# A new gate for the work that is threaded between state-space scans: own ScalarE time, due time of the next decay, and new TensorE figures in the planner

## Chip, core and metric

The kernel runs on one core of a Trainium2 chip. The metric is device time in microseconds (us) of one execution; the median of three runs is used, and 0.3% is about the least difference that they can tell. A core has TensorE (matrix products into PSUM), VectorE, ScalarE (functions by table) and GpSimd; SyncE issues the DMAs. Each engine takes its instructions in the order in which the program gives them and waits at each for what it needs, so an instruction that waits also holds up all those behind it.

## The reference

Four layers act on four images of 96 channels and 64 x 64 pixels (4096 positions).

- Layer 0: layer norm, projection to 2 x 192 channels, a 3 x 3 depthwise convolution with silu, then a selective scan of 192 channels x 16 states in 4 directions (by rows, by columns, and both backwards), the sum of the four, a layer norm, a gate, a projection, and an MLP with gelu.
- Layer 1: group norm, a smaller convolution and scan in two directions with one state a channel, gate, projection.
- Layer 2: a Fourier transform along the positions with a pointwise complex layer, and an MLP with its values rounded to FP8.
- Layer 3: linear attention (no softmax) and the same MLP.

The scan of layer 0 is where most of the time goes. Cut to what matters:

```python
dt = softplus(x_dbl[dt rows] @ dt_projs_w + bias);  A = -exp(A_logs)
def step(hst, inp):                          # for every position, in order
    dA = exp(dt_t[..., None] * A)            # the decay
    hst = hst * dA + dt_t[..., None] * B_t * x_t[..., None]
    y_t = sum over the 16 states of hst * C_t
```

## The kernel before

**Tiles of the scan.** A tile holds 32 channels x 4 states on 128 partitions and 1024 positions. For 4 images, 4 directions (in the order 0, 1, 3, 2), 4 chunks of 1024 positions and 24 tiles a chunk there are 1536 tiles. In `scan` (from line 655) the work on tile i is spread over the engines:

- GpSimd multiplies u by B into `w` (`input_of`, L745), three tiles ahead; there are nine `w` buffers.
- ScalarE makes the decay exp(dt A) into `h` (`decay`, an activation whose trace line is L144), two tiles ahead; there are two `h` buffers.
- VectorE runs the scan (L821), with `h` and `w` as inputs.
- The product with C is done on VectorE (L829) for most tiles and on GpSimd (L841) for 5 of 24 tiles of image 0 and 8 of 24 of the others (`POOL_OUT`, `pool_out`). The last state is copied by ScalarE (L837) or GpSimd (L834).
- TensorE sums over the states, for two tiles at once (`sums`, L767, into `py`), and VectorE adds `py` to `y` once in eight tiles (`add_sums`, L779 and L782).

**The stream.** All the other layers are written as generators, which end each of their steps with `yield`: `front(b)` (layer norm, convolution, step sizes of layer 0, stored in DRAM for the scan), `weights`, and `rest(b)`, which is `tail` (end of layer 0), `l1`, `transform`, `middle` and `back`. They stand in one queue, `stream`, and `step()` runs the front one to its next `yield`. `run` takes tasks in groups of w; beside the scan w is 1, so one task is in flight. It waits until 8 us (`LANDED`) of planned time have passed since the loads of a group were issued. `rest(b)` is queued when the last direction of image b begins, and its tail can take a part of the image only when that direction's scan has passed it. `need` runs steps without a gate when the scan needs a front that isn't there.

**The planner.** The order of instructions is fixed while the program is built. `now` holds the planned time of each engine and `chain` the planned end of the stream's last work on it. `spend` charges a stream operation to an engine behind what it needs, and `tick` charges the scan's work: 2.35 us for a scan, 1.23 for a product on VectorE, 1.12 for a decay, 2.36 for GpSimd's products. An activation costs 0.25 us plus 0.86 ns for each element of a partition, and 2.6 us more where the function table changes. A matmul costs what `mm` (L97) says, divided by `side` where it fills only part of the array. `later` puts a VectorE operation of the stream off, and `flush` issues it when the planned time of VectorE has reached that of its inputs; as long as one is put off no further step is taken.

**The gate.** After the scan of a tile, and again at the end of the tile, `advance` (from line 1543) decides whether one step of the stream is run there. It compares how far TensorE's chain, ScalarE, GpSimd and TensorE are ahead of the time `free`, and takes one step if the latest is at most 2 us (first place, `FIRST`) or 1 us (second, `SECOND`) beyond it:

```python
late = max(chain["pe"] - 0.5, now["act"], now["pool"] - 6.0, now["pe"] - 2.0) - free
if not put_off and late <= slack:
    step()
```

The scan starts when the first chunk's inputs are there. When it has ended, what is left of `rest(3)` runs with eight PSUM banks and up to four tasks at once, without the gate.

Of the kernel before, what the change touches and what calls it, by code (L numbers as in the profile page):

```python
# [11 lines left out]
F32 = mybir.dt.float32  # L12
# [17 lines left out]
POOL_OUT = (5, 8, 8, 8)  # L30
# [2 lines left out]

LANDED = 8.0

FIRST, SECOND = 2, 1
ENGINES = ("pe", "act", "dve", "pool")


# [17 lines left out]
def tile_hybrid(ctx: ExitStack, tc: tile.TileContext, I: dict, out: bass.AP):  # L57
# [5 lines left out]
    now, chain = (dict.fromkeys(ENGINES, 0.0) for _ in range(2))  # L63
    done_at, used, slot_of = {}, {}, {}

    def tick(e, us, *behind):
        now[e] = max(now[e], 0.0, *behind) + us
        return now[e]

    def blocks(ap):  # L70
        t = ap.tensor
        if ap.space == DRAM:
            return []
        span = sum(abs(st) * (n - 1) for st, n in list(ap.ap)[1:])
        lo = ap.offset % int(np.prod(t.shape[1:]))
        return [(t.name, q) for q in range(lo // 512, (lo + span) // 512 + 1)]

    def spend(e, us, reads=(), writes=()):
        behind = [chain["dve"]]
        for ap in reads:  # L80
            behind += [done_at.get(q, 0.0) for q in blocks(ap)]
        for ap in writes:
            behind.append(used.get(slot_of.get(ap.tensor.name), 0.0))
        chain[e] = end = tick(e, us, *behind)
        for ap in writes:
            for q in blocks(ap):
                done_at[q] = end
        for ap in (*reads, *writes):
            if ap.tensor.name in slot_of:
                used[slot_of[ap.tensor.name]] = end  # L90

    def size(ap):
        return int(np.prod(ap.shape[1:]))

    def mm(o, lhsT, rhs, side=1, **kw):

        spend("pe", size(rhs) / side * (2.4e-3 if rhs.dtype == F32 else 1.2e-3), (lhsT, rhs), (o,))  # L97
        nc.tensor.matmul(o, lhsT=lhsT, rhs=rhs, **kw)  # L98

    dve = nc.vector  # L100
    pool = nc.gpsimd
# [30 lines left out]
    def act(o, i, func, own=False, **kw):  # L132

        if func in (AF.Exp, AF.Ln):
            if table[0] != "ln exp":
                nc.scalar.preload_act_table_set("natural_log_exp_and_others")  # L136
            table[0] = "ln exp"
        elif func in (AF.Silu, AF.Gelu, AF.Softplus):
            if table[0] != func:
                spend("act", 2.6)  # L140
            table[0] = func
        if not own:
            spend("act", 0.25 + size(o) * 0.86e-3, (i,), (o,))
        nc.scalar.activation(o, i, func, **kw)  # L144
# [17 lines left out]
    put_off = []  # L162
# [11 lines left out]
    class Now:  # L174
        ps = None
        banks = 8
        width = 1
        beside = False
        busy = False
        drain = False  # L180

    def bank(name):
        p = Now.ps.tile([128, 512], F32, tag="c", name=name)
        slot_of[p.tensor.name] = len(slot_of) % Now.banks
        return p

    def two_groups(w):

        return min(2 * w, 4)

    def run(tasks, w, ahead=1, ready=None, landed=LANDED):


        groups = [tasks[i : i + w] for i in range(0, len(tasks), w)]
        begun = []

        def load(upto):
            while len(begun) < min(upto, len(groups)) and (ready is None or ready(len(begun))):
                for t in groups[len(begun)]:
                    next(t)  # L200
                begun.append(now["dve"])

        load(ahead)
        for i, live in enumerate(groups):
            while len(begun) <= i or Now.beside and now["dve"] < begun[i] + landed:
                load(i + ahead)
                yield
            while Now.drain:
                yield
            Now.busy = True  # L210
            while live:
                load(i + 1 + ahead)
                live = [t for t in live if next(t, live) is not live]
                if live:
                    yield
            Now.busy = False
# [77 lines left out]
    def weights():  # L294
# [8 lines left out]
        def task():  # L303
# [17 lines left out]
            for h in (lo64, hi64):  # L321
                mm(pf[h, 1:2], lhsT=wraw[:, 128:192], rhs=b1, start=True, stop=True)
# [332 lines left out]
    def scan(pls, advance, need, last_pass):  # L655
# [6 lines left out]
        chunks = [(b, k, step) for b in range(B) for k in DIRS for step in range(NCH)]  # L662

        tiles = [(ci, p, g, a) for ci in range(len(chunks)) for p in range(3) for g in range(4) for a in range(2)]
        states, us, dts, bbs, ccs, hs, ws, py, y = {}, {}, {}, {}, {}, {}, {}, {}, {}
# [6 lines left out]
        def load_y(ci):  # L672
            b, k, step = chunks[ci]
            if step == 0:
                y_ds[b] = dram.tile([DI, L], F32, name=f"y_d{b}")

                y[b] = [yp.tile([128, L // 2], F32, tag=f"y{p}", name=f"y{p}") for p in range(3)]
            for p in range(3):
                for h, s in enumerate((lo64, hi64)):
                    dma(  # L680
                        y[b][p][s, step * 512 : step * 512 + 512],
                        yin_ds[b][64 * p : 64 * p + 64, step * CH + 512 * h : step * CH + 512 * h + 512],
                    )
# [29 lines left out]
        def loads(ci, x):  # L713
# [14 lines left out]
            if x == 4 and chunks[ci][1] == DIRS[0]:  # L728
                load_y(ci)

        def decay(i):
            if i >= len(tiles):
                return
            ci, p, g, a = tiles[i]
            j = 24 * chunks[ci][1] + 4 * (2 * p + a) + g
            h = hs[i] = ph.tile([128, CH], F32, tag="h", name="h")
            act(h, dts[ci, 2 * p + a], AF.Exp, own=True, scale=negA[:, j : j + 1])
            t_h[i] = tick("act", 1.12, t_out.get(i - 2, 0.0))

        def input_of(i):  # L740
            if i >= len(tiles):
                return
            ci, p, g, a = tiles[i]
            w = ws[i] = wk.tile([128, CH], F32, tag="w", name="w")
            pool.tensor_mul(w, us[ci, 2 * p + a], bbs[ci, g])  # L745
            t_w[i] = tick("pool", 2.36, t_sum.get(i - W, 0.0))
# [55 lines left out]
        for i, (ci, p, g, a) in enumerate(tiles):  # L802
            b, k, step = chunks[ci]
            x = i % 24
            loads(ci, x)
            if x == 0:
                if step == 0:
                    states[b, k] = ck.tile([128, 24], F32, tag="state", name="state")
                if step == 0 and k == DIRS[-1]:
                    last_pass(b)  # L810
            if i >= 3:
                sums(i - 3)
            input_of(i + AHEAD)

            h, w = hs.pop(i), ws[i]
            pool_out = (x * POOL_OUT[b]) % 24 < POOL_OUT[b]
            o = w if pool_out else h
            r = slice(None, None, -1) if k >= 2 else slice(None)
            j = 4 * (2 * p + a) + g
            state = states[b, k][:, j : j + 1]  # L820
            dve.tensor_tensor_scan(o[:, r], h[:, r], w[:, r], state if step else 0.0, ALU.mult, ALU.add)  # L821
            t_out[i] = tick("dve", 2.35, t_h.pop(i), t_w.pop(i))
            if i >= 4 and tiles[i - 4][2:] == (3, 1):
                add_sums(*tiles[i - 4][0:2])
            flush(now["dve"])
            advance(now["dve"] + (0.0 if pool_out else 1.2), FIRST)
            cc = ccs[ci, g]
            if not pool_out:
                dve.tensor_mul(w, o, cc)  # L829
                t_out[i] = tick("dve", 1.23)  # L830
            if step < NCH - 1:
                last = 0 if k >= 2 else CH - 1
                if pool_out:
                    pool.tensor_copy(state, o[:, last : last + 1])  # L834
                    tick("pool", 0.19, t_out[i])
                else:
                    nc.scalar.copy(state, o[:, last : last + 1])  # L837
                    tick("act", 0.16, t_out[i])
            decay(i + 2)
            if pool_out:  # L840
                pool.tensor_mul(w, o, cc)  # L841
                t_out[i] = tick("pool", 2.36, t_out[i])
            flush(now["dve"])
            advance(now["dve"] + 2.4, SECOND)
        flush()
        for i in (-3, -2, -1):
            sums(len(tiles) + i)
# [662 lines left out]
    def step():  # L1510

        while stream:
            if next(stream[0], stream) is not stream:
                return True
            stream.popleft()
        return False
# [23 lines left out]
        sb("sc", 4), sb("sb", 5), sb("sw", W), sb("sy"), psum("sh", 2), psum("sp", 1), psum("oth", 3)  # L1540
    )
    Now.ps, Now.banks, Now.beside = pls.pop(), 3, True
    def advance(free, slack):


        late = max(chain["pe"] - 0.5, now["act"], now["pool"] - 6.0, now["pe"] - 2.0) - free
        if not put_off and late <= slack:
            step()

    def need(*chunk):  # L1550
        while chunk not in there:
# [156 lines left out]
```

## Time and profile before

| | |
|---|---|
| median of the runs (lowest, highest) | 6824.64 us (6809.26, 6828.71) |
| the profiled execution: its own time | 6833.64 us |
| its span, first to last instruction | 6831.9 us, 52664 instructions |
| VectorE busy | 5603.1 us, 82% |
| GpSimd busy | 5188.9 us, 76% |
| TensorE busy (matmuls) | 4673.5 us, 68%, mean granted clock 0.743 |
| ScalarE busy | 3731.0 us, 55% |
| first scan starts, last product of the scan ends | 97.2 us, 6231.5 us |

In the profile L12 stands for line 12 of the kernel. A line of a helper such as `mm` (L98) or `act` (L144) gathers many operations, so the names of the tiles tell them apart: `out<-in`. A wait is put down to the instruction that ended it. A row of a group gives the count (x), then the busy time and the mean time in ns of one, then the idle time of the engine ahead of them and what ended it. PE is TensorE, DVE VectorE, ACT ScalarE, POOL GpSimd. `h<-dt` on ScalarE is the decay; `py<-w` on TensorE is the sum over states.

### The profile page before, as it was taken

How to read it: one execution, taken by the hardware profiler on the slowest of the kernel's cores; microseconds unless marked ns; L12 is line 12 of the kernel's file. 1: busy time of each engine (PE TensorE's matmuls, PEld its weight loads, DVE VectorE, ACT ScalarE, POOL GpSimd, SP SyncE). 2: the span in 40 equal slices, each digit the busy share in tenths (PEclk: the TensorE clock that was granted, in tenths of full speed). 3: DMA queues.
4: the chain of work that ended last, by engine and by line, in shares of the span. 5: the costliest groups of instructions: out<-in, count | busy, mean ns of one | idle time of the engine just before them, and what ended most of it. 6: DMA issues, size and time to landing. Idle time of an engine off the chain costs nothing. (4 is left out here: it accounts for less than half of the span.)

```text
span 6831.9 us, 52664 instructions
## 1 busy us (share of the span) xinstructions
PE 4673.5 (68%) x15538; PEld 1514.0 (22%) x15538; DVE 5603.1 (82%) x3872; ACT 3731.0 (55%) x5242; POOL 5188.9 (76%) x2732
## 2 busy tenths in 40 slices
PE   6758667676677666666776675657676666576877
PEld 2112111121112124211111142211111332111353
DVE  3888779797789998998899998898999989984413
ACT  3556546666555545665555455566555456553337
POOL 4888879899779788998688898897887889972000
PEclk8768677686778778766777786668777876676987
DMA  5766666767544348444443375454434563442141
GB/s 149 217 194 193 185 180 192 208 207 210 156 132 143 116 136 262 137 146 144 134 151 125 98 262 155 131 158 139 143 128 127 189 209 127 133 144 83 43 125 37
DMA packets 502464, 1050.00 MB, mean 154 GB/s; under 512 B 138448, under 2 KB 252178, under 8 KB 501144
## 3 DMA queue, kind: packets, MB, share of 16 engines
q1 hardware_dynamic: 502176, 1046.63, 49.5%
q8 instruction: 123, 2.02, 0.1%
q14 instruction: 165, 1.35, 0.1%
HBM read 831.15 MB, written 211.09 MB: 153 GB/s over the span
## 5 line engine op out<-in xcount | busy, mean ns | idle before, releaser
L745 POOL TENSOR_TENSOR w<-u,bb 128x1024 f32<-128x1024 f32 x1536 | 3587.5, 2358 | 179.5 <-PE py L767 123.8
L144 ACT ACTIVATE h<-dt,negA 128x1024 f32<-128x1024 f32 x1536 | 1706.8, 1117 | 795.6 <-DVE w L829 429.2
L821 DVE TENSOR_TENSOR_SCAN h<-h,state,w 128x1024 f32<-128x1024 f32 x804 | 1886.8, 2347 | 271.9 <-ACT h L144 202.8
L829 DVE TENSOR_TENSOR w<-h,cc 128x1024 f32<-128x1024 f32 x1072 | 1309.0, 1221 | 56.7 <-DMA cc<-bc_d 18.8
L767 PE MATMUL py<-w,idup 128*32 128x512 f32 x6144 | 1125.3, 805 | 244.1 <-POOL w L841 80.9
L841 POOL TENSOR_TENSOR w<-w,cc 128x1024 f32<-128x1024 f32 x464 | 1092.0, 2353 | 188.3 <-DVE w L821 142.4
L821 DVE TENSOR_TENSOR_SCAN w<-h,state,w 128x1024 f32<-128x1024 f32 x348 | 814.5, 2341 | 50.9 <-ACT h L144 29.2
L837 ACT COPY state<-h 128x1 f32<-128x1 f32 x804 | 127.5, 159 | 1279.4 <-DVE w L829 1278.6
L821 DVE TENSOR_TENSOR_SCAN h<-h,w 128x1024 f32<-128x1024 f32 x268 | 612.9, 2287 | 103.6 <-ACT h L144 73.5
L98 PE MATMUL pc<-xp 97*64 97x512 f32 (+1 forms) x1152 | 400.2, 611 | 12.4 <-DMA xp<-wc_d 7.8
L767 PEld LDWEIGHTS py<-w,idup 128*32 128x32 f32 x6144 | 164.5, 126 | 1057.3 <-issue 597.3
L834 POOL COPY state<-w 128x1 f32<-128x1 f32 x348 | 64.3, 185 | 363.9 <-DVE w L821 363.1
L111 POOL TENSOR_TENSOR u<-dt,xi 128x512 f32<-128x512 f32 x160 | 216.8, 1371 | 156.7 <-ACT dt L144 142.3
L821 DVE TENSOR_TENSOR_SCAN w<-h,w 128x1024 f32<-128x1024 f32 x116 | 264.4, 2279 | 71.9 <-POOL w L745 55.1
L98 PE MATMUL pc<-xp,wc 96*96 96x512 f32 x576 | 275.1, 631 | 25.6 <-ACT u L144 25.6
L98 PE MATMUL pd<-xd,dtw 6*64 6x512 f32 (+1 forms) x512 | 211.4, 983 | 92.8 <-ACT xd L148 59.1
L98 PE MATMUL pcen<-t,cen 96*96 96x512 f32 x192 | 137.5, 853 | 161.3 <-POOL t L1332 78.8
L144 ACT ACT_TABLE_LOAD x176 | 225.8, 1283 | 32.0 <-PE pd L98 18.1
L136 ACT ACT_TABLE_LOAD x174 | 223.2, 1283 | 3.8 <-PEq L1698 0.7
L98 PEld LDWEIGHTS pc<-xp 97*64 97x64 f32 (+1 forms) x1152 | 149.9, 167 | 270.2 <-issue 239.4
L98 PE MATMUL po<-hq,q 128*96 128x512 fp8e5 x192 | 88.7, 586 | 163.0 <-POOL hq L1320 132.1
L98 PE MATMUL pvar<-sq,avg 96*96 96x512 f32 x256 | 168.9, 801 | 45.3 <-ACT sq L144 45.3
(242 smaller groups left out, 6330.8 us busy)
## 6 DMA issues: line engine op xcount, KB each, us to landing
u<-u_d SPq DMA_DIRECT2D x384, 512.0 KB
dt<-dt_d SPq DMA_DIRECT2D x384, 512.0 KB
bb<-bc_d SPq DMA_DIRECT2D x256, 512.0 KB
cc<-bc_d SPq DMA_DIRECT2D x256, 512.0 KB
dt_d<-dt SPq DMA_DIRECT2D x128, 256.0 KB
u_d<-u SPq DMA_DIRECT2D x128, 256.0 KB
f_d<-fo SPq DMA_DIRECT2D x64, 384.0 KB
a<-f_d SPq DMA_DIRECT2D x64, 384.0 KB
```

The source lines that it names most:

```text
L98: nc.tensor.matmul(o, lhsT=lhsT, rhs=rhs, **kw)
L111: aside(0.2 + size(o) * 2.1e-3, o, a, b).tensor_mul(o, a, b)
L136: nc.scalar.preload_act_table_set("natural_log_exp_and_others")
L144: nc.scalar.activation(o, i, func, **kw)
L745: pool.tensor_mul(w, us[ci, 2 * p + a], bbs[ci, g])
L767: nc.tensor.matmul(o, lhsT=idup, rhs=v, **flags)
L821: dve.tensor_tensor_scan(o[:, r], h[:, r], w[:, r], state if step else 0.0, ALU.mult, ALU.add)
L829: dve.tensor_mul(w, o, cc)
L834: pool.tensor_copy(state, o[:, last : last + 1])
L837: nc.scalar.copy(state, o[:, last : last + 1])
L841: pool.tensor_mul(w, o, cc)
```

## The change

The gate gets another rule, and the planner other TensorE figures. The operations themselves stay the same; their order in the engines' queues changes.

- `spend` adds every ScalarE charge to `Now.spent`. `run` notes for each step of each kind of task (by the task function's name and the step's number) how much ScalarE time it charged (`known`), and puts the figure for the coming step into `Now.next`: 2.0 where it isn't known yet, 0 at a task's end.
- `advance(until)` gets the planned time by which ScalarE must begin the next decay: the end of the scans and VectorE products ahead of the scan that needs it (`by(i)` is 1.23 us, or 0 where GpSimd has tile i's product), less 1.3 us. A step is taken if ScalarE, or TensorE's chain where that is later, plus the step's own ScalarE time ends at most 1.0 us after `until` (`SPARE` is -1.0). GpSimd may be up to 10 us and TensorE up to 5 us ahead of VectorE (`POOLAG`, `LAG`). For a step with no ScalarE time TensorE's chain doesn't count.
- The gate goes on taking steps at one place until it refuses, a VectorE operation is put off, or a step moves no engine's planned time.
- `mm` charges 1.2e-3 us an element for F32 instead of 2.4e-3, and 0.9e-3 for other types instead of 1.2e-3.

```diff
-FIRST, SECOND = 2, 1
+SPARE, LAG, POOLAG = -1.0, 5.0, 10.0
...
+        if e == "act":
+            Now.spent += us
         chain[e] = end = tick(e, us, *behind)
...
-        spend("pe", size(rhs) / side * (2.4e-3 if rhs.dtype == F32 else 1.2e-3), (lhsT, rhs), (o,))
+        spend("pe", size(rhs) / side * (1.2e-3 if rhs.dtype == F32 else 0.9e-3), (lhsT, rhs), (o,))
...
             Now.busy = True
+            at = 0
             while live:
                 load(i + 1 + ahead)
+                key = (live[0].__name__, at)
+                before = Now.spent
                 live = [t for t in live if next(t, live) is not live]
+                known[key] = Now.spent - before
+                at += 1
+                Now.next = known.get((key[0], at), 2.0) if live else 0.0
                 if live:
                     yield
...
+        def by(i):
+
+            n = POOL_OUT[chunks[min(i, len(tiles) - 1) // 24][0]]
+            return 0.0 if i % 24 * n % 24 < n else 1.23
...
-            pool_out = (x * POOL_OUT[b]) % 24 < POOL_OUT[b]
+            pool_out = by(i) == 0.0
...
-            advance(now["dve"] + (0.0 if pool_out else 1.2), FIRST)
+
+            advance(now["dve"] + by(i) + 2.35 + by(i + 1) - 1.3)
...
-            advance(now["dve"] + 2.4, SECOND)
+
+            advance(now["dve"] + 2.35 + by(i + 1) + 2.35 + by(i + 2) - 1.3)
...
-    def advance(free, slack):
-
-
-        late = max(chain["pe"] - 0.5, now["act"], now["pool"] - 6.0, now["pe"] - 2.0) - free
-        if not put_off and late <= slack:
-            step()
+    def advance(until):
+
+
+        t = now["dve"]
+        while not put_off:
+            through = max(now["act"], chain["pe"]) + Now.next if Now.next else now["act"]
+            if through > until - SPARE or now["pool"] > t + POOLAG or now["pe"] > t + LAG:
+                return
+            before = list(now.values())
+            if not step() or before == list(now.values()):
+                return
```

More of the change, by code (lines that the diff above doesn't have):

```diff
@@ L178, in tile_hybrid @@
         beside = False
+        spent = 0.0
+        next = 0.0
         busy = False
@@ L185, in bank @@
         return p
+    known = {}
     def two_groups(w):
```

## The prediction

> **What bounds the kernel now.** I read four views, coarse to fine. First the busy times of the stretch that the change can touch, from the first scan of the state (97 us) to the last (6232 us). The columns are stretch, length, then busy time of TensorE, its weight loads, VectorE, ScalarE and GpSimd, then the granted clock, the DMA share and GB/s:
>
> ```profile
> 97.00:6232.00 6135.00, 4173.23 (x13804) 1274.93 (x13804) 5433.55 (x3618) 3441.33 (x4763) 5171.75 (x2706) 0.74 0.52 162
> ```
>
> VectorE is the bound: busy 5433.6 of 6135 us, which leaves 701 us. The change adds no VectorE work and removes none, so only these 701 us can shrink or grow. GpSimd, at 5171.8 us, is second. The second view is VectorE's list of waits in this stretch (who waited, for whom, us in total, times, longest):
>
> ```profile
> DVE h L821 <- ACT h L144: 276.2, 144, 13.5
> DVE y L779 <- PE py L767: 68.1, 27, 6.7
> DVE y L782 <- PE py L767: 62.9, 16, 15.9
> DVE w L821 <- POOL w L745: 56.1, 7, 51.0
> DVE h L821 <- POOL w L745: 49.9, 37, 3.0
> DVE h L821 <- ACT state L837: 44.2, 26, 7.2
> DVE w L821 <- ACT state L837: 33.2, 11, 13.0
> DVE w L821 <- ACT h L144: 33.0, 17, 7.1
> ```
>
> Scans wait for the decay or for a state copy, both on ScalarE: 276.2 + 44.2 + 33.2 + 33.0 = 386.6 us in 198 waits, mean 1.95 us. Sums that are late on TensorE cost 131.0 us. GpSimd's 106.0 us include the 51.0 us before the very first scan, so 55 us are at stake. The gate aims at the 386.6.
>
> Why is ScalarE late? The third view is one such place in order of time, the layer-0 tail: TensorE's instructions, then ScalarE's, then the scan that suffered (start, length, instruction, idle time before it and its cause):
>
> ```profile
> 1888.30 2.08 PE L98 MATMUL pca<-ya,cenr 128*128 128x512 f32 x2
> 1890.30 2.07 PE L98 MATMUL pca<-yb,cenr 64*128 64x512 f32 x2
> 1892.31 1.97 PE L98 MATMUL pcb<-ya,cenr 128*64 128x512 f32 x2
> 1894.20 1.97 PE L98 MATMUL pcb<-yb,cenr 64*64 64x512 f32 x2
> 1896.10 1.97 PE L98 MATMUL pcb<-ya,cenr 128*64 128x512 f32 x2
> 1898.00 1.97 PE L98 MATMUL pcb<-yb,cenr 64*64 64x512 f32 x2
> ```
>
> ```profile
> 1892.41 0.60 ACT L144 ACTIVATE sa<-pca 128x512 f32<-128x512 f32 x1 [0.78 <-PE pca L98]
> 1900.00 0.60 ACT L144 ACTIVATE sbb<-pcb 128x512 f32<-128x512 f32 x1 [6.99 <-PE pcb L98]
> ```
>
> ```profile
> 1902.88 2.35 DVE L821 TENSOR_TENSOR_SCAN w<-h,state,w 128x1024 f32<-128x1024 f32 x1 [5.36 <-ACT h L144]
> ```
>
> ScalarE stood 6.99 us behind matmuls of the stream with the decay queued after it, and the scan lost 5.36 us. TensorE took 1888.3 to 1900.0 = 11.7 us for what the planner books (old rates) as two matmuls of 1.23 and four of 0.61, 4.9 us. So the planner's TensorE figures decide such waits. The fourth view, two rows of the page's groups, shows what a matmul costs:
>
> ```profile
> L98 PE MATMUL pc<-xp 97*64 97x512 f32 (+1 forms) x1152 | 400.2, 611 | 12.4 <-DMA xp<-wc_d 7.8
> L98 PE MATMUL pc<-xp,wc 96*96 96x512 f32 x576 | 275.1, 631 | 25.6 <-ACT u L144 25.6
> ```
>
> The code issues 18 matmuls in each of 16 layer-1 convolutions, 288; the row counts 576. An F32 matmul is two records. The 611 ns of one record is what 1.2e-3 us x 512 = 0.614 us books for a whole matmul; 275.1 / 288 = 0.96 us is what it costs. FP8 is one record (192 `po<-hq` rows for 192 matmuls, mean 586 ns), and 0.46 us is a little short.
>
> **What the Trainium skill says.** "FP8 and Floating Point Precision", section "TensorE Precision Notes": true FP32 takes four passes through the array; "TensorE: Matmul & The Clock Gate", section "Wait — 56ns, not 53.3ns?", gives 215.7 ns start to start for 512 columns warm. An estimate from both is 0.86 us a matmul. The trace agrees with its 0.96 us at a granted 0.74, and disagrees with 0.614. "ScalarE: Activation LUTs", section "What ACT_TABLE_LOAD costs", gives 1283 ns and a drain of some 1380. The trace has 1283 ns for its 350 loads and the next ACTIVATE starts 1.29 us after a load's start, so no drain shows; the 2.6 us that the planner books stand for two loads, there and back (2.57).
>
> **The change, part by part.** It adds and removes no engine operation or DMA; the order of ScalarE, TensorE, GpSimd, VectorE and SP queues around the scan changes. Stream DMAs move with their steps, and the scan's loads may stand behind them on SP. Before, the only `cc` wait was 18.8 us once; I book nothing, up to 20 us if three more of those arise.
>
> *A. Own ScalarE time (gain).* Before, a step started with ScalarE up to 2 us beyond the free time, whatever it cost: a softplus or silu step books 3 x 0.69 + 2.6 = 4.67 us. Now it must fit: `until` is 1.3 us ahead of the scan, SPARE lets it pass by 1.0, the decay takes 1.118 us, so a planned decay is late by at most 1.0 + 1.118 - 1.3 = 0.82 us. More places are now filled up to this limit, so waits don't vanish. I take the 198 waits from 1.95 to 1.25 us: -140 us. Ends: 0 (each saved wait replaced by a smaller, more frequent one) and -250 us.
>
> *B. TensorE's rates (loss).* F32 drops to half, to about 0.6 of the real cost. Consumers of a matmul are then put into the in-order ScalarE and VectorE queues before it is done, ahead of a decay or scan. Measured against booked, per unit of the stream after the first scan:
> - Layer-0 convolution: 400.2 / 16 = 25.0 us, booked 18 x 0.614 + 18 x 0.307 = 16.6 (33.2 before). 8.4 us short; half is taken up by the nine w buffers and GpSimd's lead. 15 x 4 = +60 us.
> - Layer-1 convolution: 17.2 against 11.1 us (22.1 before). 12 x 2.5 = +30.
> - Tail tasks: the rows pz, pca, pcb, pv, po, pcen, pvar, ph and pm give 47 us a task, booked 20.3 (40.6 before). The old shortfall of 6 becomes 27. But its 4.67 us steps fit only where two scans in a row have their product on VectorE (one tile in three), which leaves gaps that catch most of it up. I pass on a fifth: 15 x 4 = +60.
> - Normalisations outside the tail: pcen 137.5 / 48 + pvar 168.9 / 64 = 5.5 us against 2.46, 3 us short, 0.9 passed on, some 60 of them: +54.
> - Projections px and pd: (180.0 + 213.6) / 32 = 12.3 us against 5.3. A sixth of the 7 us, 30 of them: +36.
>
> Sum +240 us, between +60 (nearly all caught in gaps) and +500. The sum waits (131.0 us) are in the first two lines: with LAG at 5 and halved rates, TensorE's real queue runs longer before `add_sums`.
>
> *C. Several steps at a place, POOLAG 10.* The loop stops once ScalarE, TensorE or GpSimd is too far ahead, and on any pending VectorE operation. GpSimd's old limit was its time up to 8 to 9.4 us ahead; now 10. Zero, from -10 (less to force at the thirteenth tile, where the 13.0 us wait above lies) to +40. A faster stream ends nothing sooner: the tail of an image needs its last scan direction, and already the last hidden cast of image 2 ends well before the last scan at 6227.9 us:
>
> ```profile
> L1320 POOL CAST hq<-h x24: 1026/1036/1053, 2776.5 to 5994.5; 128x1024 fp8e5<-128x1024 f16 x24
> ```
>
> These 230 us are the reserve; a slower stream costs nothing until it is gone.
>
> Opening (97 us) and closing part (600 us) call the stream without a gate: nothing. The sum is -140 + 240 + 0 = +100 us on the profiled execution of 6833.6 us (span 6831.9), 6934 us. The median of the runs is 9.0 us lower; 6925 us.
>
> **Rivals.**
> *Gate wins (faster).* One mechanism: margins left by steps that don't fit catch TensorE's shortfall, so B is +60, A is -140: 6745 us. For it: most waits are 1 to 2 us, the size of a margin, and the stretch from 513 to 684 us, with convolutions in it, has TensorE busy 137.8 of 171 us and VectorE still at 151.6. Against it: where the planner was short by 7 us (the place above), 5.36 us came through. It decides at a pass-on of some 0.6 of what I take.
> *Shortfall passes on in full measure.* B at +480: TensorE becomes the bound while the stream runs, and the tiles it leaves empty cannot give that back; 6825 - 140 + 480 = 7165 us. For it: the same place; against it: the w buffers and TensorE's 68% busy.
> *No difference.* The stream is one chain of dependent steps with w = 1; the new order then only moves waits: 6825 us, A and B cancelling.
> *Stream too slow.* If the 4.67 us steps starve, image 2's back spills into the closing part: past the 230 us reserve, each us of it costs nearly one. From 400 us late, +170. I give it 3 in 100, inside the second rival.
>
> **How the numbers follow.** My forecast (6840 to 7030 us) 0.42; gate wins 0.32; full shortfall 0.18; no difference 0.08. Under 0.3% (20 us) a measurement of this kernel can't tell a change. Slower 0.42 + 0.18 = 0.60, same 0.08, faster 0.32. A third of "gate wins" lies under 6690 us and half of the full shortfall above 7110 us: the range is 6690 to 7110.
>
> **What would show it.** A right: waits of scans for the decay shorter on the mean, longest below 10 us. B right: ScalarE's waits for pcb, px, pcen and VectorE's for py grow, and the tail's stretch has more idle VectorE; total VectorE idle near 800 us. Wrong if the 386.6 us fall under 250 and py stays near 131. C right: last hq cast of GpSimd earlier than 5994 us, closing part still 600 us.

## The result, and the profile after

The changed kernel takes 7192.0 us (median of 4 runs, 7185.8 to 7203.9) against 6826.7 us (6809.3 to 6830.1): ratio 1.0543, 95% interval 1.0519 to 1.0566. It is 365 us slower. The forecast had the sign and the cause, but the time lies 82 us above the top of the range.

First the busy times by stretch, of the kernel after (columns as in the first view of the prediction): the scans, the closing part, one of three stretches that have no like before, and the scans of images 0 and 1.

```profile
98.00:6580.00 6482.00, 4263.38 (x13798) 1316.98 (x13798) 5453.22 (x3619) 3458.61 (x4766) 5170.68 (x2706) 0.71 0.49 153
6580.00:7186.00 606.00, 462.34 (x1622) 225.71 (x1622) 164.97 (x242) 266.38 (x443) 1.55 (x8) 0.79 0.26 75
6110.00:6263.00 153.00, 54.90 (x200) 8.20 (x192) 151.54 (x87) 56.23 (x64) 152.26 (x74) 0.57 0.44 150
98.00:1840.00 1742.00, 1280.37 (x3694) 340.97 (x3694) 1340.68 (x832) 987.24 (x1322) 1354.44 (x730) 0.71 0.62 185
1840.00:3416.00 1576.00, 988.47 (x3368) 322.18 (x3368) 1370.53 (x930) 823.01 (x1148) 1273.35 (x661) 0.71 0.45 143
```

Nearly the whole loss is in the scans: 6482 us where before had 6135. VectorE's busy time is the same within 20 us (5453.2 against 5433.6), so its idle time went from 701 to 1029 us. The closing part is unchanged (606 against 600).

For comparison, image 0 of the kernel before:

```profile
97.00:1642.00 1545.00, 1106.32 (x3439) 297.41 (x3440) 1302.14 (x788) 896.45 (x1197) 1326.45 (x713) 0.73 0.66 198
```

Image 0 lost 197 of the 347 us (1545 to 1742); images 1, 2 and 3 lost 60, 29 and 62. In image 0, 125 more ScalarE instructions (1322 against 1197) and 174 us more of TensorE's busy time stand than before: the stream was brought forward. In each of images 1 to 3 it then has nothing left to do in two chunks of 24 tiles, since the tail can't begin before the first chunk of the image's last direction has been scanned. The stretch from 6110 to 6263 us is such a pair: VectorE idles 1.5 us in 153 and GpSimd 0.7, and the other engines keep up. A chunk takes 75 to 78 us there, against 96 us on the mean of the kernel before (6135 / 64), which has no chunk without stream. But no chunk can be shorter than VectorE's own work, or GpSimd's, which is as long here; so it wins back little: images 1 to 3 lose time too, though a part of their stream's work is already done.

VectorE's list of waits in the scans of after (who, for whom, us, times, longest):

```profile
DVE h L838 <- ACT h L146: 323.5, 120, 16.8
DVE w L838 <- ACT h L146: 147.6, 17, 51.5
DVE y L799 <- PE py L784: 124.7, 32, 9.7
DVE y L796 <- PE py L784: 108.8, 35, 10.5
DVE w L838 <- ACT state L855: 63.1, 26, 10.7
...
DVE xr L969 <- PE po L100: 31.4, 26, 3.2
...
DVE h L838 <- ACT state L855: 26.0, 20, 5.0
```

The 51.5 us are the wait before the very first scan, which stood under GpSimd before. Without it, scans waited for ScalarE 323.5 + 96.1 + 63.1 + 26.0 = 508.7 us in 182 waits, before 386.6 in 198: fewer waits, but a mean of 2.79 us where before had 1.95. Sums late on TensorE cost 233.5 us (131.0 before). VectorE's own stream instructions, such as the `xr` row, waited 165 us (59 before). The three rises, 122 + 103 + 106, come to 331 us and so account for the 328 us, small waits apart. (The view leaves out waits under 150 ns; sums over all scans, as in the table of the experiments, differ from it by 1 or 2 us.)

The same place of the tail as in the prediction, there in image 0's tail, here in image 1's and in the kernel after: TensorE, then ScalarE, then the scan (start, length, instruction, idle time before it and its cause).

```profile
3243.22 2.07 PE L100 MATMUL pca<-ya,cenr 128*128 128x512 f32 x2 [1.03 <-ACT za L146]
...
3251.23 1.97 PE L100 MATMUL pcb<-ya,cenr 128*64 128x512 f32 x2
...
3258.81 1.93 PE L784 MATMUL py<-w,idup 128*32 128x512 f32 x8
```

```profile
3251.33 0.60 ACT L146 ACTIVATE sa<-pca 128x512 f32<-128x512 f32 x1 [1.72 <-PE pca L100]
3258.92 0.60 ACT L146 ACTIVATE sbb<-pcb 128x512 f32<-128x512 f32 x1 [6.99 <-PE pcb L100]
```

```profile
3261.60 2.36 DVE L838 TENSOR_TENSOR_SCAN h<-h,state,w 128x1024 f32<-128x1024 f32 x1 [8.21 <-ACT h L146]
```

Eight matmuls from 3243.2 to 3258.8 us, 15.6 us; the new charges book 4 x 0.614 + 4 x 0.307 = 3.7. ScalarE has `sbb` queued, stands 6.99 us behind `pcb`, and the decay behind it is late: the scan loses 8.21 us, where the place before lost 5.36. ScalarE's own wait is 6.99 us in both. What differs is how much work VectorE still had when it began: 4.5 us before, 1.5 us here. Over the whole kernel, ScalarE's waits for TensorE grew where the prediction looked for it:

```profile
ACT sq L146 <- PE pcen L100: 208.3, 72, 32.4
ACT g L146 <- PE px L100: 100.9, 83, 25.8
ACT sbb L146 <- PE pcb L100: 100.9, 16, 7.0
```

Before they were 110.4, 46.8 and 69.4 us. And GpSimd's products of the scan stood behind the w buffers, which TensorE frees late: 370.9 us of waits for `py`, 123.8 before.

### The profile page after: what moved, and what is told of

Its sections match the earlier page's. It is cut to its first block, busy times and chain, and to the rows that moved or that the text cites. A ratio compares the mean times of both kernels' runs of the same rounds, so it can differ in the third digit from the quotient of the medians.

```text
span 7185.2 us, 52743 instructions
## 1 busy us (share of the span) xinstructions
PE 4769.9 (66%) x15538; PEld 1558.3 (22%) x15538; DVE 5622.1 (78%) x3872; ACT 3748.8 (52%) x5245; POOL 5187.6 (72%) x2732
## 5 line engine op out<-in xcount | busy, mean ns | idle before, releaser
L762 POOL TENSOR_TENSOR w<-u,bb 128x1024 f32<-128x1024 f32 x1536 | 3585.1, 2357 | 409.3 <-PE py L784 370.9
L784 PE MATMUL py<-w,idup 128*32 128x512 f32 x6144 | 1198.7, 821 | 706.8 <-POOL w L859 210.8
L100 PE MATMUL pc<-xp,wc 96*96 96x512 f32 x576 | 251.0, 594 | 0.0
L796 DVE TENSOR_TENSOR y<-y,py 128x512 f32<-128x512 f32 x96 | 114.8, 1196 | 108.9 <-PE py L784 108.8
L146 ACT ACTIVATE dt<-pd,vec 128x512 f32<-128x512 f32 (+1 forms) x256 | 162.0, 684 | 61.3 <-DMA dt_d<-dt 57.1
```

What stands on the lines that cost most here:

```text
L784: nc.tensor.matmul(o, lhsT=idup, rhs=v, **flags)
L796: dve.tensor_add(v, v, s.rearrange("p (w a r) -> p w a r", w=16, a=4))
```

## The experiments

All times are medians, and each ratio is to the kernel before on the same chip (6821 to 6832 us). "Scan" is the stretch from the first to the last scan, "closing" what follows, "idle" VectorE's idle time in the scans after the first (gaps over 50 ns); "ScalarE" and "py" are scans waiting for the decay or a state, and late sums. All from the profiled execution.

| kernel | us | ratio (95%) | scan | closing | idle | ScalarE | py |
|---|---|---|---|---|---|---|---|
| before | 6826.7 | 1 | 6134 | 600 | 673 | 388 | 131 |
| the change | 7192.0 | 1.0543 (1.0519 to 1.0566) | 6482 | 605 | 1001 | 509 | 234 |
| new charges alone | 7226.4 | 1.0579 (1.0554 to 1.0603) | 6535 | 602 | 1063 | 668 | 196 |
| new gate alone | 7032.0 | 1.0297 (1.0274 to 1.0319) | 6136 | 786 | 722 | 379 | 171 |
| change, one step a place | 7071.3 | 1.0353 (1.0324 to 1.0383) | 6386 | 602 | 917 | 427 | 257 |
| change, F32 at 1.9e-3 | 6978.9 | 1.0229 (1.0195 to 1.0263) | 6293 | 584 | 833 | 407 | 208 |
| that, one step a place | 6954.6 | 1.0180 (1.0148 to 1.0211) | 6137 | 725 | 711 | 276 | 227 |
| old gate, F32 at 1.9e-3 | 6964.4 | 1.0192 (1.0158 to 1.0226) | 6262 | 601 | 789 | 476 | 140 |
| change, LAG 2 | 7102.7 | 1.0396 (1.0360 to 1.0432) | 6412 | 599 | 936 | 497 | 189 |
| change, F32 at 1.9e-3, LAG 2 | 6898.6 | 1.0096 (1.0064 to 1.0128) | 6180 | 617 | 733 | 350 | 175 |
| old gate, charges by kind | 6821.4 | 0.9983 (0.9971 to 0.9995) | 6135 | 603 | 664 | 413 | 125 |
| change, charges by kind | 6980.2 | 1.0205 (1.0167 to 1.0244) | 6156 | 731 | 732 | 348 | 173 |
| that, SPARE -2, LAG 3.5 | 6973.5 | 1.0205 (1.0172 to 1.0238) | 6262 | 602 | 779 | 426 | 181 |
| that, SPARE -3, LAG 2 | 6877.5 | 1.0070 (1.0042 to 1.0097) | 6162 | 613 | 712 | 332 | 212 |
| by kind, one step, SPARE -3, LAG 3.5 | 6795.4 | 0.9957 (0.9941 to 0.9972) | 6101 | 603 | 638 | 388 | 128 |
| old test and own time, by kind, one step | 6810.6 | 0.9980 (0.9967 to 0.9994) | 6100 | 615 | 646 | 354 | 114 |

### The change taken apart

**The charges alone, with the old gate.**

```diff
-        spend("pe", size(rhs) / side * (2.4e-3 if rhs.dtype == F32 else 1.2e-3), (lhsT, rhs), (o,))
+        spend("pe", size(rhs) / side * (1.2e-3 if rhs.dtype == F32 else 0.9e-3), (lhsT, rhs), (o,))
```

> The kernel before with nothing changed but the TensorE charges (1.2e-3 and 0.9e-3). Theory R: most of the loss appears, 7030-7220 us, with stretches of scan tiles that hold no stream work. Theory G: within 100 us of before, under 6930 us.

Measured 7226.4 us, ratio 1.0579, some 400 us slower: just above the band, and more than the whole change costs. So one line of figures that no engine ever sees makes more than the entire loss. VectorE's waits in the scans of this kernel (98 to 6633 us):

```profile
DVE h L821 <- ACT h L144: 400.6, 130, 13.8
DVE h L821 <- ACT state L837: 116.0, 59, 14.3
DVE w L821 <- ACT h L144: 105.5, 32, 10.9
DVE y L779 <- PE py L767: 98.7, 25, 8.8
DVE y L782 <- PE py L767: 97.4, 23, 9.0
```

Scans wait 667 us for ScalarE (388 before), in 240 waits. Three chunks without stream stand in it too.

**The gate alone, with the old charges.**

```diff
-        spend("pe", size(rhs) / side * (1.2e-3 if rhs.dtype == F32 else 0.9e-3), (lhsT, rhs), (o,))
+        spend("pe", size(rhs) / side * (2.4e-3 if rhs.dtype == F32 else 1.2e-3), (lhsT, rhs), (o,))
```

> The changed kernel with the TensorE charges of before (2.4e-3 and 1.2e-3 us an element); gate, own ScalarE time and several steps at a place as changed. Theory R (the halved charges cost the time): VectorE's idle time in the scan falls back to 700 us or less and the kernel to 6750-6930 us; the closing part may grow past 600 us, since the stream is then planned slower and some of it can be left over when the scan ends. Theory G (the new gate itself, or filling several steps into a place, costs it): 7080 us or more.

Measured 7032.0 us: a miss. The scans take 6136 us, as before, but the closing part grew from 600 to 786 us. The row of hidden casts in this kernel says why:

```profile
L1339 POOL CAST hq<-h x20: 1035/1037/1049, 2998.6 to 6189.0; 128x1024 fp8e5<-128x1024 f16 x20
```

Only 20 of 24 ran under the scans, the last of them some 45 us before these end at 6235 us. With the full charges the new test lets too few steps in; the rest of the stream runs behind the last scan, where nothing hides it. That is the rival that the prediction gave 3 in 100 ("stream too slow"), real, but not what happened in the change: there the row reads

```profile
L1339 POOL CAST hq<-h x24: 1026/1036/1050, 2572.9 to 6063.7; 128x1024 fp8e5<-128x1024 f16 x24
```

with all 24 under the scans and the last of them started 516 us before the last scan ends.

**At most one step at a place, all else as changed.**

```diff
-            before = list(now.values())
-            if not step() or before == list(now.values()):
-                return
+            step()
+            return
```

> The changed kernel, but at most one step of the stream at a place, as before. Theory R: still 7080 us or more. Theory S (several steps at a place crowd the queues): under 6950 us.

Measured 7071.3 us, 121 us faster than the change, between the two theories. Its list of waits, in the scans:

```profile
DVE h L838 <- ACT h L146: 275.4, 108, 12.4
DVE y L799 <- PE py L784: 141.2, 31, 11.9
DVE y L796 <- PE py L784: 115.4, 33, 10.4
DVE w L838 <- ACT h L146: 105.5, 15, 51.4
DVE h L838 <- ACT state L855: 71.9, 19, 12.8
...
DVE w L838 <- ACT state L855: 24.8, 9, 10.6
```

Against the charges alone, which differ from it by the gate's test (own ScalarE time, due time and the limits `LAG` and `POOLAG` together): ScalarE's share falls from 667 to 426 us (without the 51.4 of the first scan), in 150 waits where there were 240. The mean stays at 2.8 us. The sums' share rises by 60 us. So the three parts, put in one after the other, are: charges +400, the new test -155, several steps at a place +121 us; together 365. The order counts: with the old charges the whole gate costs 205 us instead of saving anything.

The 121 us don't lie in the sums, whose share is 257 us with one step and 234 with several. What grew with several steps is ScalarE's share (427 to 509 us) and the waits of VectorE's own stream instructions (121 to 165 us). ScalarE's waits for `pcen` ahead of `sq`, which are 208.3 us in the change, are 119.9 us here.

Scan lengths by image, in us, with the difference to before:

| kernel | image 0 | image 1 | image 2 | image 3 |
|---|---|---|---|---|
| before | 1545 | 1516 | 1548 | 1524 |
| charges alone | 1760 (+215) | 1590 (+74) | 1594 (+46) | 1589 (+65) |
| change, one step | 1718 (+173) | 1586 (+70) | 1542 (-6) | 1538 (+14) |
| the change | 1742 (+197) | 1576 (+60) | 1577 (+29) | 1586 (+62) |

Whatever the gate, more than half of the loss with the low charges falls in image 0, during which the fronts of the other images are in the queue, so that the stream never lacks work.

### How much the charges are to blame

**F32 at 1.9e-3, the measured 0.96 us of a long run (0.96 / 512), in the change; then also one step a place; then in the old gate.**

```diff
-        spend("pe", size(rhs) / side * (1.2e-3 if rhs.dtype == F32 else 0.9e-3), (lhsT, rhs), (o,))
+        spend("pe", size(rhs) / side * (1.9e-3 if rhs.dtype == F32 else 0.9e-3), (lhsT, rhs), (o,))
```

> The changed kernel with an F32 charge of 1.9e-3 us an element, 0.97 us for 512 columns, which is what 275.1 us over 288 matmuls of the layer-1 convolution give; 0.9e-3 for FP8 kept. Theory R: 6700-6850 us, since the plan is then near what TensorE does and the gate's gain on ScalarE shows. Theory G: 7080 us or more.

> The changed gate with the F32 charge of 1.9e-3 and at most one step at a place. With the charges near right, what is left of the loss (6979 against 6827 us) is put to the test. Theory S (several steps at a place put TensorE work of the stream ahead of the sums): the scan's stretch falls by 80 us or more, VectorE's waits for py fall to 150 us or less, and the closing part grows, since the own-time rule lets fewer steps pass; in all 6880-6980 us. Theory O (the own-time rule itself, not the number of steps): the stretch stays within 40 us of 6293 us.

> The kernel before with charges of 1.9e-3 for F32 and 0.9e-3 for FP8 and nothing else. If the loss grows evenly with the shortfall of the charge (1.2e-3: 7226 us; 2.4e-3: 6827 us), 6930-7030 us. If only charges well below the real cost hurt, under 6870 us.

Measured 6978.9, 6954.6 and 6964.4 us. The first is 213 us faster than the change, yet missed its band from above: much of the loss stays. With one step a place the scans fall by 156 us to 6137, but 141 us of it come back in the closing part (584 to 725 us), from the same starving as with the gate alone; the sums' share, expected at 150 us or less, did not fall (227 us). In the old gate, 2.4e-3 gives 6827, 1.9e-3 gives 6964, 1.2e-3 gives 7226 us (the other charge is 1.2e-3 in the first and 0.9e-3 in the other two): in the band for a loss that grows evenly with the shortfall. So the figure that the layer-1 convolution shows is still worse than the high one.

The trace says why: that figure is not the mean of the stream's matmuls. In the scans of the kernel before, TensorE is busy 4173 us, 1125 of them with the sums, so the stream's matmuls take about 3050 us. Added up over these same matmuls as the program is built, the planner books 3136 us with the figures of before, 2475 us with 1.9e-3 and 0.9e-3, and 1612 us with the changed ones. The high figure has hardly a reserve, taken over all of them; the two low ones are some 570 and 1440 us short and cost some 135 and 400 us, about a quarter of that (an estimate from these figures). Why the convolution's matmuls are the quick ones is shown in the last section.

**Charges by kind, in the old gate.** F32 at 1.85e-3; a matmul that starts behind a wait in the plan is charged 1.0 us more, since the matmuls of the tail's groups above take 2 us each where the convolution's take 0.96; and two kinds of half-width products, the tail's `pcb` and the inverse transform's, are no longer booked at half.

```diff
+        if e == "pe" and max(behind) > now[e]:
+            us += 1.0
...
-        spend("pe", size(rhs) / side * (2.4e-3 if rhs.dtype == F32 else 1.2e-3), (lhsT, rhs), (o,))
+        spend("pe", size(rhs) / side * (1.85e-3 if rhs.dtype == F32 else 0.9e-3), (lhsT, rhs), (o,))
...
-                centred(pb[h], 1, cenr[:, 0], cenr[h, 1], ya[:, j], yb[h], 2)
+                centred(pb[h], 1, cenr[:, 0], cenr[h, 1], ya[:, j], yb[h])
...
-                            lhsT=gt[h, m, j * C : (j + 1) * C], rhs=mi2[h], side=2, start=True, stop=True,
+                            lhsT=gt[h, m, j * C : (j + 1) * C], rhs=mi2[h], side=0.7, start=True, stop=True,
```

> The kernel before with TensorE's charges nearer to the trace than either: F32 1.85e-3 and FP8 0.9e-3 us an element, 1.0 us more for a matmul that finds TensorE idle in the plan, no division by two for the half-array products of the tail, and the inverse transform's 64-column products at 0.17 us. If shortfalls in the charges are what costs time, the tail's and the inverse transform's waits shrink and it is at or under before: 6760-6830 us. If it is only the lower average that hurts, 6880 us or more.

Measured 6821.4 us, ratio 0.9983: as expected. The charge per F32 element is close to the 1.9e-3 that cost 2%, the FP8 charge is the same 0.9e-3, and the loss is gone. But the edit also brings back the total: 589 matmuls beside the scans are charged the 1.0 us more, and the planner books 3073 us, close to the 3050 that TensorE takes. So the run doesn't tell a plan that is too low at some places (the tail's short groups, half-width products, products that start late) from one that is too low in all. What speaks for the total: the figures of before spread nearly the same total otherwise (763 us on the convolutions, which take 590, where this run books 602), and the two kernels are within 0.2%.

### The lead that TensorE is given

**LAG 2 in place of 5, in the change, and in the change with F32 at 1.9e-3.**

```diff
-SPARE, LAG, POOLAG = -1.0, 5.0, 10.0
+SPARE, LAG, POOLAG = -1.0, 2.0, 10.0
```

> The change as it is, with LAG 2 in place of 5. At charges of half the cost a limit on the planned lead is worth half: theory R expects a part of the loss back, 7060-7150 us, the rest staying with the charges. If the loose limit on TensorE's lead were the main thing, it is under 6950 us.

> The changed gate with several steps at a place and the F32 charge of 1.9e-3, with LAG 2 in place of 5: TensorE may be 2 us ahead of VectorE. Theory S: VectorE's waits for py fall from 208 us to under 160 us and the kernel to 6900-6950 us. Theory O: no more than 20 us from 6979 us.

Measured 7102.7 (-89 us) and 6898.6 (-80 us). The first is in its band; the second is 1.4 us below it, and its sums' share (175 us) stayed above the 160 that were expected. For a step that has no ScalarE time the new test doesn't look at TensorE's chain, so LAG is what bounds TensorE there. With LAG at 5 TensorE may be 5 us ahead in the plan, which is more in truth where the charges are too low, and the sums, the w buffers and then GpSimd stand behind it. With LAG 2 the sums' share falls from 234 to 189 and from 208 to 175 us, and GpSimd's waits for `py` from 370.9 to 301.2 and from 236.0 to 173.2 us.

### Is the own-time test worth having?

**The change with charges by kind, at three settings.** The edit is that shown for the old gate; the second and third set SPARE and LAG besides.

```diff
-SPARE, LAG, POOLAG = -1.0, 5.0, 10.0
+SPARE, LAG, POOLAG = -2.0, 3.5, 10.0
```

> The changed gate, all of it (several steps, LAG 5, SPARE -1), with the charges by kind that brought the old gate to 6821 us. If the charges are the cause of the loss, the stretch of the scan is no longer than before (6134 us) and only a longer closing part stays, since this gate then passes fewer steps: 6830-6930 us. If the new gate has a loss of its own, the stretch stays above 6220 us.

> Charges by kind, changed gate with SPARE -2 and LAG 3.5, so that the stream keeps pace: the closing part back at about 600 us, ScalarE's own time still counted: 6780-6850 us if the own-time rule is worth its 60 us, 6860 us or more if several steps at a place take them away.

> As the one before with SPARE -3 and LAG 2: TensorE held closer, ScalarE freer. Closing part near 600 us; waits for py under 140 us; 6760-6840 us if TensorE's lead is what is left of the loss.

Measured 6980.2, 6973.5 and 6877.5 us. The first and the third missed upwards; the second lies where several steps at a place take the gain away. The first has short scans (6156 us) and a leftover (closing 731 us): with these charges SPARE -1 starves the stream. At SPARE -2 and LAG 3.5 the leftover is gone and the scans take 106 us more. I had thought that the charges alone would mend the change; they don't.

**One step a place as well, SPARE -3, LAG 3.5.**

```diff
-            before = list(now.values())
-            if not step() or before == list(now.values()):
-                return
+            step()
+            return
```

> Charges by kind, changed gate with at most one step at a place, SPARE -3 and LAG 3.5, so that the stream keeps the pace of before. If several steps at a place are what is left of the loss, the stretch of the scan is at or under 6134 us with the closing part near 600 us: 6740-6830 us. If the own-time rule has no worth of its own, 6840 us or more.

Measured 6795.4 us, ratio 0.9957 (0.9941 to 0.9972), in its band, and faster than both kernels: 26 us under the kernel before in the same comparison (6821.4). The scans are 34 us shorter, the sums are as early as before (128 us), and no chunk is without stream. Against the old gate with the same charges (0.9983) the gain is 0.26%, some 18 us, and the two intervals just meet; LAG and POOLAG differ too, so it isn't the test's alone.

**The old test kept, the own-time test added.** One step a place, charges by kind, SPARE -3.

```diff
-        if not put_off and late <= slack:
+        through = max(now["act"], chain["pe"]) + Now.next if Now.next else now["act"]
+        if not put_off and late <= slack and through <= until - SPARE:
             step()
```

> Charges by kind, the old gate's test kept whole, and the own-time test (SPARE -3) added to it, one step at a place. It can only refuse more than the old gate. If steps that overrun the decay by their own ScalarE time cost what my prediction put on them, 6700-6790 us; if ScalarE is late for TensorE's sake, within 30 us of 6821 us.

Measured 6810.6 us, ratio 0.9980 (0.9967 to 0.9994), where the same charges with the old test alone gave 0.9983 (0.9971 to 0.9995): nothing that can be told apart. Its scans wait 354 us for ScalarE, where those charges alone have 413, but its closing part is 12 us longer. Of the runs it is the nearest to term A by itself, and there it is worth nothing that shows. SPARE -3 is a looser limit than the change's -1, though; what a tight one is worth where it doesn't starve the stream, no run shows.

How much of ScalarE's lateness comes from its own work can be read from the traces as well. For each scan that waited for ScalarE, I took ScalarE's stream instructions of the 6 us before the wait and how long they themselves stood, and for whom; up to that time the scan's wait counts for that engine, and the rest as ScalarE's own work. It is a division that I worked out, not a view:

| scans' waits for ScalarE, us | own work | behind TensorE | behind DMA |
|---|---|---|---|
| before | 149 | 212 | 16 |
| charges alone | 169 | 453 | 36 |
| the change | 90 | 336 | 73 |
| one step, by kind, SPARE -3 | 149 | 166 | 67 |

(What is left to the totals has other causes.) The new test does what it says: 169 to 90 us. But that is the smaller part; the halved charges more than double the larger one. In the change with one step a place, the two parts are by the same rule some 95 and 285 us: the new test, which looks at TensorE's chain too, takes more off the waits behind TensorE than off ScalarE's own work.

## Why the prediction was right or wrong

**Right: the sign and the mechanism.** VectorE is the bound, and only its idle time could move: the busy time moved by 20 us, the idle time by 328. The F32 matmul as two records, and with it charges that book half a matmul, is the cause: the charges alone cost 400 us, in the places foretold: in that kernel ScalarE's waits for `pcb`, for `px` (ahead of `g`) and for `pcen` (ahead of `sq`) are 97.4, 104.5 and 130.9 us, before 69.4, 46.8 and 110.4, and VectorE's for `py` 196 against 131. The closing part was left alone. One reading beside it was wrong: the prediction sets the 0.96 us of the layer-1 convolution beside a granted clock of 0.74, which is the mean of all the scans. That convolution's matmuls had 0.94; at 1.00 they take 0.86 us, as the prediction's estimate has it. And 0.96 us is not what an F32 matmul costs elsewhere: outside the convolutions it is about 1.2 us for 512 columns on the mean (an estimate: some 2330 of the 3050 us above, over 1.00 million elements as the planner counts them).

**Wrong in size: step B, +240 us, where the charges alone cost 400.** The step that failed is the sum over the units. The shortfalls in its list come to some 990 us; over all of the stream's matmuls beside the scans, TensorE takes about 1440 us more than is booked. Products of the transform (`px<-a`, `px<-g`, `ph<-w,xa`) and of the small scan (`pB`, `pC`) are not in it. The shares passed on (a half, a fifth, a sixth) were chosen, not read, and were nearer: together 240 / 990 = 0.24, where 400 / 1440 = 0.28 was passed on. By this estimate the same shares of the whole would have given some 350 us, so the larger part of the miss is what the list left out. The list also took each unit's shortfall by itself. What the runs show is a stream that the plan runs ahead of what TensorE can do in image 0 (+215 us of the 400 with the charges alone), and whole chunks without stream later, in which VectorE and GpSimd already run at their floor of 75 us and give little back. The prediction says this of its second rival, "the tiles it leaves empty cannot give that back", but priced only that rival with it. Its 7165 us is 27 us from the result, by luck: its +480 us is called full measure, but is half of the list's own 990, and it has nothing for step C. Its other half, TensorE as the bound, is not what happened: TensorE is busy 66% of the scans and 73% in image 0.

**Wrong: step C, booked at 0, measured +121 us.** I argued that the limits on ScalarE, TensorE and GpSimd would end the loop as the old test did, and that a faster stream ends nothing sooner. The second is right (the last hidden cast has 516 us in hand where it had 233). The first failed: inside those limits, several steps at a place lengthen the scans' waits for ScalarE (427 to 509 us) and those of VectorE's stream instructions (121 to 165 us); the sums' share does not grow with them (257 to 234 us). Which of the steps let in do it is not shown. The limits themselves were too wide for charges that book too little: LAG 2 in place of 5 takes 80 to 89 us off, of which the sums' share gives 33 to 45.

**Half right: step A, -140 us.** At the changed charges, with one step a place, the new test is worth 155 us, close to the 140. That is luck in good part. More of it came off the waits behind TensorE than off ScalarE's own steps, which were what the term was about, and it came as fewer waits (240 to 150), not as shorter ones (2.8 us in both); I took 198 waits as given, and their length as what changes. The sign named in advance, a longest wait under 10 us, did not show (16.8). And the gain isn't the test's to give in general: it is there because the charges make ScalarE late. With charges by kind it is 0 to 18 us with SPARE at -3, and the gate as changed with the old charges is 205 us slower than before, since the stream starves.

**The rivals.** "Gate wins" needed A whole and B at 60; B at 400 ends it. "No difference" fell too. "Shortfall passes on in full" was nearest, at 0.18. Of the error of 267 us, 160 are B, 121 are C, and A gave back 15.

**What stays open.** Whether it matters at which places the plan is too low, beside how low it is in all. Why image 0 takes the larger part: its stream is that of layer 0, with convolutions and 4.67 us softplus steps, and it never lacks work; which of the two counts isn't told apart. Nor is LAG apart from POOLAG in the best kernel.

## What to carry to other kernels

A planner's durations are part of the kernel: halving the F32 figure and lowering the other by a quarter, with no instruction changed but in its place in the queues, cost 5.8%. Count the records of an operation before a record's mean is booked as its time; take the figure from all the operations that it will stand for, not from the row that is easiest to read; and add up what the plan books against what the engine was busy. And a gate that lets more work in is priced by what it lets stand before the bound engine's suppliers, not by the limits that it checks in its own plan.

## What the runs showed of the hardware

The time of an F32 matmul goes with the granted clock, the share of TensorE's full clock that the profile shows it to have had. At any one moment it is either 1.00 or 0.50 in these traces; other figures are means. Two stretches of the kernel before, with columns as in the first view of the prediction: 72 matmuls of the layer-1 convolution in the closing part (144 records; the view counts two more at its edges), and the tail's place that the prediction shows.

```profile
6337.70:6399.50 61.80, 61.80 (x146) 23.41 (x145) 0.00 (x0) 5.64 (x9) 0.00 (x0) 1.00 0.08 26
1882.40:1901.80 19.40, 19.37 (x33) 3.59 (x33) 14.98 (x9) 9.38 (x16) 11.36 (x6) 0.50 0.84 236
```

At 1.00 a matmul takes 61.8 / 72 = 0.86 us, at 0.50 those of the tail take 2 us. The same product differs as much between its places: `pca` takes 1.06 us at 1.00 and 2.01 at 0.50, `pcb` 1.00 and 1.90 (medians from start to start). The convolutions' matmuls had a mean clock of 0.94 (layer 1) and 0.98 (layer 0), those of the rest of the stream 0.71. So a time that is read from one row holds for the clock which that row had.

Whether a half-width F32 product takes half the time depends on how it is issued. In the tail's place, where the two halves of `pcb` come one after the other, a matmul with 64 columns of weights takes 1.97 us, `pca` with 128 takes 2.07 (at a clock of 1.00 it is 1.00 against 1.06): booking `pcb` at half was wrong in the kernel before too. In the layer-0 convolution the half-width matmuls start in pairs, within 0.01 us of each other, and 288 of them take 130.6 us, where 288 of full width take 269.7: there half is right.

The granted clock in the stretches without stream was 0.57, against 0.71 over the scans (54.9 of 153 us busy, against 4263 of 6482); it cost nothing there, with VectorE idle 1.5 us in 153. Nor did the lower clock (0.71 in the scans after, 0.74 before) slow the stream's matmuls: without the sums, TensorE is busy 3065 us in the scans after and 3048 before. The sums' own busy time rose from 1125 to 1199 us.
